# A convolution, a weighted sum over 49 neighbours and a whitening: weight loads on another queue, the sums of two images one gap later, and two softmaxes in another form

## The chip, the cores and the metric

The kernel runs on one core of a Trainium2 chip. It computes in float32. The metric is the device time of one execution in microseconds (us). Five engines work side by side, each on its own list of instructions in order: TensorE (PE: matmuls and transposes), VectorE (DVE), ScalarE (ACT), GpSimd (POOL) and SyncE (SP, which only issues DMAs). SP, ACT and POOL each can issue DMAs.

## The reference

Cut to what matters; x is (4, 256, 64, 64), so there are four images of 256 channels. They are counted 0 to 3 in this document, as the program does.

```python
# layer 0
k = conv(x, w1, padding=6, rhs_dilation=2) + b1         # 7x7, dilated by 2: 256 -> 128 channels
k = conv1x1(k, w2) + b2                                 # 128 -> 49
attn = softmax(k, axis=1)                               # 49 weights for each pixel
xp = pad(x, 6)
y[b,c,h,w] = sum over u,v in 0..6 of xp[b, c, h+2u, w+2v] * attn[b, 7u+v, h, w]
# layer 1: whitening of y, in 4 groups of 64 channels
Sigma = EPS*I + (yc @ yc.T) / m                         # yc: y less its mean over images and pixels
rTr = 1 / trace(Sigma);  P = I
for _ in range(5):
    P = 1.5*P - 0.5 * (P @ P @ P) @ (Sigma * rTr)
out = (P * sqrt(rTr)) @ yc * weight + bias
```

## The kernel before, in words

**Convolution.** The two convolutions of layer 0 have no function between them, so the kernel convolves with 49 outputs. It does so by evaluating input and weights at points and multiplying there, much as a Winograd algorithm does. The image is worked through in six row steps (`br` 0 to 5) with three banks each, by `conv_step`. A bank is one stretch of matmuls into PSUM (`conv_bank`, L599: 96, 80 and 32 matmuls in the three banks of a row), with operand `xh` (input values at the points) and weights `wr`. VectorE makes `rb`, `ct` and `xh` out of the image (L347, L350, L354, a few on ACT at L547), ACT copies the result out of PSUM into `pv` (L610, L615), and VectorE interpolates `pv` to `zz` and to the logits `lgx`. Weights at the points are made once and kept in DRAM (`gd`); every later image loads them back with `weights` (L419), 42 loads in all: 14 each of 588, 490 and 196 KB. Each of the three tags `wr0` to `wr2` has one buffer, so a load waits until the matmuls that used the last weights in it are done.

**Softmax.** `softmax(b, pc)` works on one image's pixels of one column parity `pc`. PE transposes the logits (L990), so that pixels lie on partitions; VectorE takes the maximum over 49 (L996) and turns its sign (L999). Then there are two forms. For images 0 to 2, ACT does 16 exps of 128x49 (L1016) with the maximum as bias and a sum as second output, which is an instruction of its own (ACTIVATION_READ_ACCUMULATOR). For image 3, VectorE adds the negated maximum (L1005, two instructions), ACT does two exps of 128x392 (L1012) and VectorE sums (L1013, two). In both, VectorE takes the reciprocal (L1020), masks it (L1022), multiplies (L1029) and shifts the terms between partitions with four shuffles (L1034).

**Weighted sums.** The sum over 49 neighbours is a matmul with a banded matrix for each of 16 pieces of work, n = 0 to 15, four for each image. `move_terms` copies the softmax terms into `zt` (on ACT, L1075, for images 0 to 2, and on VectorE, L1087, for image 3); POOL writes `zt` to DRAM (`sd`, L1092, eight DMAs); `load_band` reads it back on SP's queue as a band (L1127 `band`, L1138 `bandz`). `first_half(n)` and `second_half(n)` transpose blocks of the image (L1168), copy them out of PSUM (`xb` L1174, `xbz` L1182), multiply (`y`, L1210), store `y` (L1228 on VectorE, L1230 on ACT), turn it (L1241, copied by L1249 into `yt`), and add its moments for the whitening (`sig`, L1262). The copies of `xb` and half of the stores go to VectorE once the convolution of the last image is done (`tail`), and to ACT or by turns before.

**Order.** PE's order is that of the program. The convolution of image b + 1 has `NPC = 8` gaps, spread evenly by cost over its banks. `plan(b, j, f)` puts a piece of work into gap j of image b's convolution, and gaps past 7 run over into the next image or, behind the last, into the tail. Gaps 0 and 1 hold the two parts of the softmax of the image before. The eight halves of the sums of images 0 and 1 begin at gap 2 (past it for the following image), those of images 2 and 3 at gap 3. What is left at the end of the convolution of image 3 runs in the tail, in order. The other engines' lists are ordered by the scheduler of the framework, by its own estimates and by priorities. Layer 1's whitening and the output (`whiten`, L1594, L1610, L1561, L1563, L1598) follow the last sum.

The lines that set where things go:

```python
        if not first:
            nc.sync.dma_start(wt, gd[br][:, s0 : s0 + ns])          # weights(), L419
...
    for b in range(B):
        for j in range(2) if b else ():
            plan(b + 1, j, lambda b=b, j=j: soft(b, j))
```

Of the kernel before, what the change touches and what calls it, by code (L numbers as in the profile page):

```python
# [32 lines left out]
def kernel(  # L33
# [29 lines left out]
    nc = tc.nc  # L63
    B, C, H, W = x.shape
# [8 lines left out]
    NCH = SH // CR  # L73
# [21 lines left out]
    def taps(b):  # L95
        return (0,) if b == INF else (0, 1)
# [12 lines left out]
    def tp():  # L109
        return ps_tp.tile([P, 512], F32, tag="tp", name="tp")  # L110
# [72 lines left out]
    t = tp()  # L183
# [3 lines left out]
    t = tp()  # L187
# [4 lines left out]
    cv_buf = []  # L192
    for k in range(2):
        t = ps_cv.tile([P, 512], F32, name=f"cv{k}")
# [53 lines left out]
    for k, c0 in enumerate(range(0, P, CB)):  # L248
        n = min(CB, P - c0)
        t = cv_buf[k % 2]  # L250
# [15 lines left out]
    for k0 in range(0, KT, TB):  # L266
        n = min(TB, KT - k0)
        t = tp()
# [44 lines left out]
    for b in ORDER:  # L313
        slot_of[b] = nsl
        nsl += len(taps(b))
    gd = [
        dram.tile([P, nsl, NSK * len(taps(b)) // 2], F32, name=f"gd{b}") for b in range(NP)
    ]
# [27 lines left out]
    def add(o, a, b):  # L346
        return in_turn(TT(o, a, b, ALU.add))  # L347
# [57 lines left out]
    def weights(b, br, i, mid=None):  # L405

        first = (br, i) not in made
        made.add((br, i))
        s0 = slot_of[BANKS[i][0]]
        ns = sum(len(taps(bc)) for bc in BANKS[i])
        nk = NSK * len(taps(br)) // 2
        wt = apool.tile([P, ns, NSK], F32, tag=f"wr{i}", name=f"wr_{b}_{br}_{i}")[:, :, :nk]
        w = {bc: wt[:, slot_of[bc] - s0 : slot_of[bc] - s0 + len(taps(bc))] for bc in BANKS[i]}
        if not first:
            nc.sync.dma_start(wt, gd[br][:, s0 : s0 + ns])  # L419
            return w  # L420

        if br in kept:


            f = lgx if br == 4 else rb[0].rearrange("p q r c w -> p (q r c w)")
            f = f[:, : KS * nk]
            if i == 0:
                nc.sync.dma_start(f, kept[br])
            f = f.rearrange("p (v a r k) -> p v a r k", v=KS, a=NCC, k=KT)
            g = [f[:, v] for v in range(KS)]  # L430
        else:
            g = [gbr[:, v] for v in range(KS)]
        g = [t.rearrange("p a r k -> p (a r k)") for t in g]

        e = ct.rearrange("p a b -> p (a b)") if b else store[4].rearrange("p c r w -> p (c r w)")
        e, o, e1 = (e[:, k * nk : (k + 1) * nk] for k in range(3))
        g0 = [g[KS - 1 - a] for a in range(4)]
        g1 = [g[KS - 5 - a] for a in range(3)]
        o0 = {bc: w[bc][:, 0] for bc in w}
        o1 = {bc: w[bc][:, 1] for bc in w if bc != INF}  # L440

        def same(o, a):
            if br in kept:
                v = KS - 1 - a
                nc.sync.dma_start(o, kept[br][:, v * nk : (v + 1) * nk])
            else:
                nc.scalar.copy(o, g[KS - 1 - a])

        if i == 0:
            add(e, g0[0], g0[2])  # L450
            add(o, g0[1], g0[3])
            add(e1, g1[0], g1[2])
            add(o0[1], e, o)
            sub(o0[2], e, o)
            add(o1[1], e1, g1[1])
            sub(o1[2], e1, g1[1])
            same(o0[0], 0)
            same(o1[0], 4)
        elif i == 1:
            madd(e, g0[2], 4.0, g0[0])  # L460
            madd(o, g0[3], 4.0, g0[1])
            madd(e1, g1[2], 4.0, g1[0])
            madd(o0[3], o, 2.0, e)
            madd(o0[4], o, -2.0, e)
            madd(o1[3], g1[1], 2.0, e1)
            madd(o1[4], g1[1], -2.0, e1)
            same(o0[INF], 3)
        else:
            madd(o0[5], g0[0], 2.0, g0[1])
            madd(o1[5], g1[0], 4.0, g1[2])  # L470
            madd(o0[5], o0[5], 2.0, g0[2])
            if mid is not None:
                mid()
            madd(o1[5], g1[1], 2.0, o1[5])
            madd(o0[5], o0[5], 2.0, g0[3])
            add(o1[5], o1[5], o1[5])
        for bc in BANKS[i]:
            f = SCALE[bc] * (SCALE[br] if br not in kept else 1.0)
            if f != 1.0:
                nc.scalar.mul(w[bc], w[bc], f)  # L480
        nc.sync.dma_start(gd[br][:, s0 : s0 + ns], wt)
        return w
# [480 lines left out]
    NI = NCH // 2  # L963
# [16 lines left out]
    def softmax(b, pc):  # L980

        lv = logits[b].rearrange("p r w -> p (r w)")
        nm = f"{b}_{pc}"
        mx = work.tile([P, NCH, 2], F32, tag="mx", name=f"mx_{nm}")
        lt = []
        for hf in range(2):
            lt.append(tp().rearrange("p (i h k) -> p i h k", i=NI, h=2))
            for i in range(NI):
                pe(
                    nc.tensor.transpose(  # L990
                        lt[hf][:, i].rearrange("p h k -> p (h k)")[:, :K2],
                        lv[:K2, bass.ds(2 * (NI * hf + i) * P + pc, P, 2)],
                        ident[:K2, :K2],
                    )
                )
            nc.vector.tensor_reduce(  # L996
                mx[:, NI * hf : NI * (hf + 1)], lt[hf][:, :, :, :KT], AX.X, ALU.max
            )
        nc.vector.tensor_scalar(mx, mx, -1.0, None, ALU.mult)  # L999
        d = terms[b, pc] = bpool.tile([P, 2, NCH, KT], F32, tag="d", name=f"d_{nm}", bufs=2)  # L1000
        s = work.tile([P, 2, NCH], F32, tag="s", name=f"s_{nm}")
        if b == B - 1:
            for hf in range(2):
                half = slice(NI * hf, NI * (hf + 1))
                nc.vector.tensor_tensor(  # L1005
                    d.rearrange("p h i k -> p i h k")[:, half],
                    lt[hf][:, :, :, :KT],
                    mx[:, half].unsqueeze(3).to_broadcast([P, NI, 2, KT]),
                    ALU.add,
                )  # L1010
            for h in range(2):
                nc.scalar.activation(d[:, h], d[:, h], AF.Exp)  # L1012
                nc.vector.tensor_reduce(s[:, h], d[:, h], AX.X, ALU.add)  # L1013
        for h in range(2):
            for i in range(NCH) if b < B - 1 else ():
                nc.scalar.activation(  # L1016
                    d[:, h, i], lt[i // NI][:, i % NI, h, :KT], AF.Exp,
                    bias=mx[:, i, h : h + 1], accum_out=s[:, h, i : i + 1],
                )
            nc.vector.reciprocal(s[:, h], s[:, h])  # L1020
            rm = work.tile([P, NCH, KS], F32, tag="rm", name=f"rm_{nm}_{h}")
            nc.vector.tensor_tensor(  # L1022
                rm,
                s[:, h].unsqueeze(2).to_broadcast([P, NCH, KS]),
                cmask.unsqueeze(1).to_broadcast([P, NCH, KS]),
                ALU.mult,
            )
            dh = d[:, h].rearrange("p i (u v) -> p i u v", u=KS)
            nc.vector.tensor_tensor(  # L1029
                dh, dh, rm.unsqueeze(2).to_broadcast([P, NCH, KS, KS]), ALU.mult  # L1030
            )
        dv = d.rearrange("p h i (u v) -> p (h i u) v", u=KS)
        for step, vs in ((1, slice(4, 7, 2)), (2, slice(5, 7)), (-1, slice(0, 3, 2)), (-2, slice(0, 2))):
            last = nc.vector.stream_shuffle(  # L1034
                dv[:, :, vs], dv[:, :, vs], [(c - step) % SW for c in range(SW)]
            )

        return last
# [112 lines left out]
    tail = []  # L1151
# [177 lines left out]
    def bands(n, after=None):  # L1329

        move_terms(n, after)
        if n - 1 in half_done:
            load_band(n, 0)
        if n - 1 in done:
            load_band(n, 1)
            move_terms(n + 1, after)
# [26 lines left out]
    def plan(b, j, *what):  # L1363
        todo.setdefault((b + j // NPC, j % NPC), []).extend(what)

    def soft(b, pc):
        with tc.high_priority() if pc == 0 else nullcontext():
            last = softmax(b, pc)
        soft_done.add((b, pc))
        if pc == 0 and b == 0:  # L1370
            bands(0)

    for b in range(B):
        hs = [
            (lambda n=n, f=f: f(n))
            for n in range(4 * b, 4 * b + 4)
            for f in (first_half, second_half)
        ]
        if b + 2 < B:
            for j in range(8):  # L1380
                plan(b + 1, 2 + j, hs[j])
                if j == 3:

                    plan(b + 1, 2 + j, finish)
        else:
            for j in range(8):
                plan(b + 1, 3 + j, hs[j])
    for b in range(B):
        for j in range(2) if b else ():
            plan(b + 1, j, lambda b=b, j=j: soft(b, j))  # L1390
# [6 lines left out]
    for b in range(1, B):  # L1397
# [13 lines left out]
        j, at, whole = 0, 0, sum(c for c, _ in steps)  # L1411
# [242 lines left out]
```

## Time and profile before

| | |
|---|---|
| median of 3 runs (lowest, highest) | 739.77 us (734.72, 740.28) |
| the profiled execution: time, span | 736.93 us, 735.2 us |
| PE busy | 687.0 us, 93% of the span |
| VectorE busy | 594.5 us, 81% |
| ScalarE busy | 332.6 us, 45% |
| POOL busy | 133.2 us, 18% |
| convolution matmuls L599 | 234.1 us, 4160 of them |
| mean granted clock of PE | 0.974 |
| softmax of image 1 begins on PE | at 322.9 us of the span |
| softmax of image 2 begins on PE | at 469.0 us |
| convolution of image 3 ends on PE | at 562.0 us |

All stretches of time are in us from the start of the span. In a timeline row the first number is the start, the second the duration of the group; "x8" are eight instructions in it; what stands in square brackets is the engine's idle time before it and what it waited for. A row with "SPq" is SP's queue, where the duration includes the waits of the DMAs issued in that row. In a row of the costliest groups, "us, ns" are the sum and the mean of one.

### The profile page before, as it was taken

The numbers are of one execution on the slowest core, as the hardware profiler recorded it, in microseconds if no ns is written. First come the engines' busy times: TensorE is split into PE (matmuls) and PEld (weight loads), VectorE is DVE, ScalarE is ACT, GpSimd is POOL, SyncE is SP. The second block draws the span as 40 slices with busy tenths as digits, with TensorE's granted clock in tenths as the row PEclk, the third lists the DMA queues.
The fourth block names the chain that finished last, engine by engine and source line by source line (L and its number), as shares of the span: only waits on it lengthen the run. The fifth ranks groups of instructions, "written<-read, shape, count | busy, mean of one in ns | idle before, by whom it ended". The sixth has DMA issues, their size and how long they took to land.

```text
span 735.2 us, 19094 instructions
## 1 busy us (share of the span) xinstructions
PE 687.0 (93%) x7728; PEld 541.8 (74%) x7728; DVE 594.5 (81%) x1280; ACT 332.6 (45%) x930; POOL 133.2 (18%) x194
## 2 busy tenths in 40 slices
PE   6999999999898999988999999899999969997996
PEld 1449543478898988877999989898998858885231
DVE  3799998995796899989886899799959796435575
ACT  1424320133655654655555446727546422232564
POOL 0002526664031020020220200202202024200000
PEclk9999999999999999999999999999999978997899
DMA  8923999984665592147755820353623145463587
GB/s 321 260 91 105 238 364 234 224 184 91 174 170 146 209 292 68 62 131 252 214 128 187 279 69 11 98 163 76 182 83 79 45 89 130 107 249 140 235 362 319
DMA packets 78336, 126.09 MB, mean 172 GB/s; under 512 B 36471, under 2 KB 58664, under 8 KB 77096
## 3 DMA queue, kind: packets, MB, share of 16 engines
q1 hardware_dynamic: 65960, 82.79, 35.2%
q0 software_dynamic: 12288, 42.08, 22.1%
q8 instruction: 61, 1.00, 0.6%
q14 instruction: 27, 0.22, 0.1%
HBM read 78.78 MB, written 52.36 MB: 178 GB/s over the span
## 4 chain that ended last, share of the span: by engine, by line
PE 37%; DVE 26%; issue 9%; ACT 9%; POOL 4%; DMA 4%; SPq 0%; POOLq 0%; ACTq 0%; DVEq 0%
PE cv L599 16%; PE y L1210 6%; PE tp L1594 4%; DVE xh L354 3%; PE sig L1262 3%; DVE pv L354 3%; POOL ahead L147 3%; PE tp L1241 3%; DVE zz L354 2%; DMA band<-sd 2%; PE tp L1168 2%; DVE rb L347 2%; DVE rb L354 1%; ACT zt L1075 1%; POOL sd L1092 1%
## 5 line engine op out<-in xcount | busy, mean ns | idle before, releaser
L599 PE MATMUL cv<-xh,wr 128*49 128x128 f32 x4160 | 234.1, 275 | 0.0
L599 PEld LDWEIGHTS cv<-xh,wr 128*49 128x49 f32 x4160 | 229.1, 125 | 3.2 <-issue 1.3
L1092 POOL DMA_DIRECT2D sd<-zt x128 | 67.3, 533 | 310.5 <-ACT zt L1075 238.4
L1210 PE MATMUL y<-band,xb 128*128 128x209 f32 x512 | 113.0, 347 | 10.3 <-DMA band<-sd 10.1
L1210 PEld LDWEIGHTS y<-band,xb 128*128 128x128 f32 x512 | 87.5, 195 | 12.1 <-DMA band<-sd 9.1
L610 ACT COPY pv<-cv 113x486 f32<-113x486 f32 (+2 forms) x60 | 25.9, 432 | 98.4 <-PE cv L599 98.2
L1249 ACT COPY yt<-tp 128x256 f32<-128x256 f32 x128 | 45.5, 377 | 50.8 <-PE tp L1241 49.8
L1241 PE MATMUL tp<-ident,slot 128*128 128x128 f32 x256 | 52.4, 301 | 4.6 <-ACT yt L1249 3.0
L354 DVE SCALAR_TENSOR_TENSOR pv<-pv 113x162 f32<-113x162 f32 x176 | 52.9, 321 | 2.4 <-ACT pv L610 1.7
L1230 ACT ACTIVATE slot<-y,pivot 128x512 f32<-128x512 f32 x53 | 36.6, 739 | 35.6 <-PE y L1210 35.6
L1168 PE MATMUL tp<-ident,slot 128*128 128x128 f32 x256 | 50.2, 300 | 2.1 <-ACT xbz L1182 1.1
L1241 PEld LDWEIGHTS tp<-ident,slot 128*128 128x128 f32 x256 | 41.3, 205 | 12.5 <-ACT yt L1249 4.4
L1168 PEld LDWEIGHTS tp<-ident,slot 128*128 128x128 f32 x256 | 40.9, 204 | 5.9 <-ACT xbz L1182 1.4
L147 POOL DMA_DIRECT2D slot<-in_x_dram x20 | 33.9, 1695 | 51.4 <-issue 47.4
L1075 ACT COPY zt<-d 32x112 f32<-32x112 f32 (+2 forms) x132 | 38.2, 290 | 10.6 <-DVE d L1034 4.7
L354 DVE SCALAR_TENSOR_TENSOR xh<-ct 128x512 f32<-128x512 f32 x40 | 26.7, 689 | 18.5 <-PE cv L599 18.4
L1262 PE MATMUL sig<-yt 128*64 128x65 f32 x1024 | 37.5, 225 | 1.9 <-ACT yt L1249 1.9
L1262 PEld LDWEIGHTS sig<-yt 128*64 128x64 f32 x1024 | 32.8, 137 | 7.9 <-issue 4.1
L1016 ACT ACTIVATE d<-tp,mx 128x49 f32<-128x49 f32 x96 | 27.5, 332 | 19.2 <-DVE mx L999 19.2
L764 PE MATMUL acc<-slot,tap 128*49 128x256 f32 (+7 forms) x224 | 34.7, 468 | 0.0
L1174 ACT COPY xb<-tp 128x256 f32<-128x256 f32 x88 | 30.7, 377 | 8.1 <-PE tp L1168 7.8
L1228 DVE TENSOR_SCALAR slot<-y,pivot 128x512 f32<-128x512 f32 x11 | 8.3, 751 | 26.6 <-ACT slot L1230 26.6
(236 smaller groups left out, 1114.1 us busy)
## 6 DMA issues: line engine op xcount, KB each, us to landing
out_dram<-out SPq DMA_DIRECT2D x32, 512.0 KB, 3.6
band<-sd SPq DMA_DIRECT2D x64, 242.0 KB, 3.4
slot<-in_x_dram POOLq DMA_DIRECT2D x20, 512.0 KB, 7.3
sd<-zt POOLq DMA_DIRECT2D x128, 77.0 KB, 2.9
wr<-gd SPq DMA_DIRECT2D x14, 588.0 KB, 4.0
wr<-gd SPq DMA_DIRECT2D x14, 490.0 KB, 4.4
ahead<-in_x_dram POOLq DMA_DIRECT2D x12, 512.0 KB, 7.5
spill<-slot POOLq DMA_DIRECT2D x3, 2048.0 KB, 7.2
```

Source lines behind the costliest of these rows:

```text
L147: queue.dma_start(o[:, cc, h], src[:, :, pr, h * SW : (h + 1) * SW])
L354: return in_turn(STT(o, a, f, b, ALU.mult, ALU.add))
L599: nc.tensor.matmul(o, wv[:, sc, sr, cc], xv[bc][:, h * NCC + cc], start=(j == 0), stop=(j == len(terms) - 1), skip_group_check=True,)
L764: nc.tensor.matmul(ps[h * HB : h * HB + KT, :, o0:o1], w[v][:, cc], rhs, start=(j == 0 and k == 0), stop=(j == len(order) - 1), skip_group ...
L1075: ins = nc.scalar.copy(o, i)
L1092: nc.gpsimd.dma_start(bass.AP(tensor=D.tensor, offset=D.offset + h * HS + g * RS, ap=[[LS, TC], [CR * RS, NCH], [1, KS * WS]],), zt[p0 : p ...
L1168: nc.tensor.transpose(t[:, cc * P : (cc + 1) * P], tile_of(xt, cc, t8, h, pc), ident)
L1210: nc.tensor.matmul(ps[:, cc, q0 : q0 + nq, c0:c1], xb[:, cc * P : (cc + 1) * P], rhs, start=(k == 0), stop=(k == len(PIECES[half]) - 1), s ...
L1230: last = nc.scalar.activation(o, i, AF.Identity, bias=pivot[:, cc : cc + 1])
L1241: nc.tensor.transpose(t[:, cc * P : (cc + 1) * P], tile_of(yt, cc, i // 2, i % 2, pc), ident,)
L1249: return nc.scalar.copy(yb.rearrange("p a g c -> p (a g) c")[:, :, :GW], t[:, :C].rearrange("p (e c) -> p e c", c=GW),)
L1262: nc.tensor.matmul(sig[g * GW : (g + 1) * GW, cc], yb[:, cc, g, :GW], yb[:, cc, g], start=(count[0] == 0 and cc == 0), stop=(count[0] == 4 ...
```

## The change

There are five edits. Weights that are loaded back are issued on ScalarE's queue and no longer on SyncE's. The softmax of images 1 and 2 takes the form that image 3 has. The transposes of image 3's softmax go into the two PSUM buffers of the convolution (`cv_buf`), and not into those of `tp`. The sums of images 2 and 3 begin one gap later. And the first part of a softmax in the tail calls `bands` right away, so that the terms of n = 12 are moved at once.

```diff
@@ weights()
         if not first:
-            nc.sync.dma_start(wt, gd[br][:, s0 : s0 + ns])
+            nc.scalar.dma_start(wt, gd[br][:, s0 : s0 + ns])
             return w
@@ softmax(b, pc)
         for hf in range(2):
-            lt.append(tp().rearrange("p (i h k) -> p i h k", i=NI, h=2))
+            t = cv_buf[hf] if b == B - 1 else tp()
+            lt.append(t.rearrange("p (i h k) -> p i h k", i=NI, h=2))
             for i in range(NI):
...
-        if b == B - 1:
+        if b > 0:
             for hf in range(2):
...
         for h in range(2):
-            for i in range(NCH) if b < B - 1 else ():
+            for i in range(NCH) if b == 0 else ():
                 nc.scalar.activation(
@@ soft(b, pc)
         soft_done.add((b, pc))
-        if pc == 0 and b == 0:
-            bands(0)
+        if pc == 0 and (b == 0 or tail):
+            bands(4 * b)
@@ plan of the sums
         else:
             for j in range(8):
-                plan(b + 1, 3 + j, hs[j])
+                plan(b + 1, 4 + j, hs[j])
```

## The prediction

> **What bounds the kernel now.** I read the page first (engines, costliest groups), then the timelines of PE, SP and DVE around each softmax, and the windows of granted clock. All sums go against the profiled execution: span 735.2 us, whole run 736.93. The three runs have median 739.77; one per cent of that, 7.4 us, is about what a measurement here can tell from no change.
>
> ```profile
> PE 687.0 (93%) x7728; PEld 541.8 (74%) x7728; DVE 594.5 (81%) x1280; ACT 332.6 (45%) x930; POOL 133.2 (18%) x194
> ...
> L599 PE MATMUL cv<-xh,wr 128*49 128x128 f32 x4160 | 234.1, 275 | 0.0
> ...
> L1016 ACT ACTIVATE d<-tp,mx 128x49 f32<-128x49 f32 x96 | 27.5, 332 | 19.2 <-DVE mx L999 19.2
> ```
>
> TensorE (PE) sets the time, and its convolution (L599) never sat idle for an operand, a weight load included. So a gain can only come from PE's few holes. The softmax of image 1 shows the first kind:
>
> ```profile
> 321.91 0.45 PE L1262 MATMUL sig<-yt 128*64 128x65 f32 x8 [0.96 <-ACT yt L1249]
> ...
> 325.41 1.02 PE L990 MATMUL tp<-ident,lgx 113*128 113x113 f32 x4 [1.90 <-ACT xb L1174]
> 326.37 12.71 PE L599 MATMUL cv<-xh,wr 128*49 128x128 f32 x208
> ...
> 343.57 0.98 PE L1210 MATMUL y<-band,xb 128*128 128x209 f32 x4 [2.50 <-DMA band<-sd]
> ```
>
> Two waits for copies that stand on ACT between zt copies (L1075), and later one for a band. The band was late because SP serves one queue in order (first number start, second duration, x4 the four loads in it):
>
> ```profile
> 311.35 23.73 SPq L419 DMA_DIRECT2D wr<-gd  x4
> 335.24 0.81 SPq L1127 DMA_DIRECT2D band<-sd  x1
> ```
>
> Four weight loads hold SP for 23.73 us, each waiting for a PSUM bank's matmuls to be done with the old weights; the band stands behind, though its data had left POOL by 327.3. At image 2 the same (23.62 us from 457.44) costs nothing: its band is wanted later. The largest hole is in the tail, at sum n = 12:
>
> ```profile
> 593.80 1.15 PE L1262 MATMUL sig<-yt 128*64 128x65 f32 x32
> ...
> 602.93 1.76 PE L1210 MATMUL y<-band,xb 128*128 128x209 f32 x4 [5.15 <-DMA band<-sd]
> ...
> 613.46 1.15 PE L1262 MATMUL sig<-yt 128*64 128x65 f32 x32
> ...
> 627.63 1.15 PE L1262 MATMUL sig<-yt 128*64 128x65 f32 x32
> ```
>
> The sig moments (L1262) are my clock for the sums. From 613.46 to 627.63 is one n without a hole: 14.2 us, 7.9 for the first half and 6.3 for the second. From 593.80 to 613.46 is one first half that took 19.66: 11.8 lost, to a band that waits for the softmax of image 3 and to the half clock that followed (the columns are length, then busy us and count of PE, PEld, DVE, ACT and POOL, then the granted clock PEclk, the DMA share and GB/s):
>
> ```profile
> 585.00:598.42 13.42, 11.25 (x116) 9.58 (x116) 13.13 (x41) 4.68 (x10) 3.83 (x8) 1.00 0.17 28
> 598.42:612.07 13.65, 7.93 (x26) 6.66 (x27) 12.04 (x44) 0.74 (x2) 7.00 (x14) 0.50 0.71 155
> ```
>
> **The change part by part.**
>
> *Softmax of images 1 and 2.* Each of four calls loses 16 exps with 16 accumulator reads on ACT (pairs start about 0.28 us apart: 4.6 us) and gets two wide exps (0.53 each) there; VectorE gets two L1005 (0.52 apart) and two L1013 (0.55): 2.1 us, 8.4 in all. The zt copies no longer stand ahead of yt and xb in the changed order, so image 1's waits (0.96 + 1.90) go, and the half clock with them: 208 matmuls took 12.71 where 112 take 6.32 at full clock in the last stretch of the conv, so 208 would take 11.74; gain 1.0. VectorE's 2 x 2.1 per image lie in its lead: in the rows after this softmax its operand was ready 8.5 to 21.6 us before PE took it. If that lead were gone, the 4.2 would be on the path.
>
> *Weight loads on ACT.* 42 loads (14 each of 588, 490 and 196 KB) leave SP. Bands are then issued when their data is there: the wait of 2.50 goes. On ACT each load stands right behind the eviction of the bank that frees its buffer, so it seldom has to wait; some also wait on the completion of an earlier band (n = 0, 4, 8, 9), and evictions and the xb, xbz and yt copies are queued behind it, for which PE waits. Only n = 0's band is late enough, and PE waits for that band anyway; at most 3 us. The trace has no weight load issued on ACT. Bounds: 0 where ACT is idle (its share is 45%) to 0.53 (POOL's L1092 row, 533 ns). I take SP's own 0.33 (median of the L419 issues), as the queue kind is nearest: 42 x 0.33 = 13.9 us on ACT, of which I put 1.9 on the path before image 3, where first halves wait for ACT's xbz for 0.7 to 1.5 us now. So by the start of image 3's conv the shift is −(0.96 + 1.90 + 1.0 + 2.50) + 1.9 = −4.5 us; bounds −6.4 and about +1.
>
> The Trainium skill ("DMA: Bandwidth & Descriptors", "Issuing engines are not separate DMA queues") speaks against this part: moving issue to another engine only saves the sequencer's issue time. By that alone the move would be worth nothing to PE, and the shift −2.0; the 23.73 us above are a wait held in the queue, and not issue time, so I keep −4.5.
>
> *Sums of images 2 and 3 one gap later.* In image 3's conv, first half 8 moves behind the convolution of bank 0 of row (3,3), and second half 9 behind the conv's end. Image 2's softmax hole there holds 0.95 + 1.59 of waits plus 1.1 of half clock (416 matmuls in 24.58 us against 23.5): 3.6 us that go. But VectorE is barely ahead here: its operands were ready at 481.9, 488.5 and 500.0, PE took them at 486.6, 491.9 and 507.3. In the new order PE comes to the last one without first half 8 (9.1 us, 496.4 to 505.5): at 498.2 − 3.6 = 494.6. VectorE, with 4.2 more softmax of which its own idle here (2.58 us on 475.29) takes most, is ready at about 501.5 (bounds 500.0, nothing paid, and 504.2, all of it). PE stalls some 7 us, ends that bank (96 matmuls, 5.4) at 506.9, then does first half 8 (8.9 without its little wait): 515.8, where it stood at 512.7 before, so +3.1 in place of −3.6. With second half 9 (6.2) behind the end, the conv ends at 562.0 + 3.1 − 6.2 − 4.5 = 554.4.
>
> *The tail, counted from the conv's end.* Before: sig of first half 12 at +51.5 (613.46 − 561.96). After: second half 9 to +6.7; first half 10 with 1.2 of waiting for copies that now stand on VectorE behind the last logits (these were ready at +10.9) to +15.8; transposes of the first softmax part to +17.2 (into the conv's PSUM, which is free). Its chain on VectorE, from the rows at 578 to 595: maximum 1.1, negation 0.2, subtraction 1.0, wait for the exp 0.8, sums 1.1, reciprocal and mask 0.65, product 1.0, a store and two copies of the sums 1.5, shuffles 2.95, one maximum of the next part 0.5, zt 2.5: 13.4, done at +30.6. POOL's eight stores (4.3) and the band (about 3.4 from issue to landing) follow: the band of n = 12 is there by +40, before it is wanted; the old 5.15 us wait goes. But in the changed order the second part follows on VectorE at once, and the copy xb of n = 11's second block stands behind its products: 0.55 + 0.18 + 1.04 + 0.8 + 1.02 + 0.66 + 0.56 = 4.8, and 0.4 for the copy, +35.8. PE (second half 10 to +23.3, transposes, begin of first half 11) wants it at +27.4: a new wait of 8.4 us, followed by half clock as after 602.93. I put sig of first half 11 at +42.4 (without the wait some 32), second half 11 at +48.7, first half 12 at +56.6. That is 5.1 more than 51.5. Bounds: 46.2 if the copies slip past the softmax, 60 if the half clock lasts its full 13.65 us again.
>
> On the clock the Trainium skill ("TensorE: Matmul & The Clock Gate", Part 1) says that full speed returns after some 3.4 us of activity; the trace agrees for image 1 (3.41 us at 0.50) and not for n = 12 (13.65 us). By the rule the tail would come about 2 us earlier.
>
> **Sum:** −4.5 + 3.1 − 6.2 + 5.1 = −2.5. After n = 12 nothing changes (64.8 of the last 75 us are PE's). 736.93 − 2.5 = 734.4; the four executions shown average 737.9, 1.0 above the profiled one, so I predict 735.
>
> **Rivals.**
> A, *faster: no new wait in the tail.* If the xb copies of n = 11 run ahead of the second softmax part, sig of first half 12 comes at +46.2, and with ACT's issues hidden (−5.5): −5.5 + 3.1 − 6.2 − 5.3 = −14, so 723. For it: the old band wait has no other cause than order, and POOL and SP have time. Against: VectorE's queue runs in order, and the copy stands behind.
> B, *slower: ACT's queue pays for the loads.* Place: first halves between the conv's banks, where PE waits for ACT (xbz) already. Price: all 42 issues on the path at 0.33 = 13.9 instead of 1.9, so −2.5 + 12 = +9.5: 746. From 0.11 us of each on the path on (1.9 + 2.5 of 42), the change loses. Against: ACT's 45%, and 15 us of exps taken from it.
> C, *VectorE becomes the bound.* All of the 8.4 us are paid instead of the 1.5: −2.5 + 6.9 = +4.4: 741. Against: the lead of 8.5 us; for: the 3.4 to 4.8 at image 3.
> D, *the loads were hidden anyway:* PE never waits for weights, and the band's 2.50 us go to another wait: about 737.
>
> **How the numbers follow.** Forecast with D 0.47, A 0.21, B 0.20, C 0.12. The forecast's own range is 728 to 743. Faster by over 1% (below 732.4): A and the lower edge of the forecast, 0.26. Slower by over 1% (above 747.2): half of B and what several of the upper bounds together give, 0.20. Within: 0.54. The range reaches from A to a little above B: 722 to 748.
>
> **What would show it.** In the profile after: no L419 issue on SP beside the first ones; bands issued within 1 us of their data; no wait of PE for yt or xb above 0.5 us at image 1's softmax; PE stalled for VectorE's xh in row (3,3) of image 3, some 7 us; no band wait at n = 12; a wait for xb (L1174, VectorE) of some 8 us at n = 11 with half clock after it. The forecast is wrong if that last wait is missing (A), if PE's waits for ACT copies in first halves grow by over 5 us in total (B), or if L599 shows waits for xh in image 2's rows (C).

## The result, and the profile after

The change makes the kernel a little slower: 739.93 us against 737.52 (medians of 20 runs each), a ratio of 1.0032 with a 95% interval of 1.0016 to 1.0047. The forecast was 735, which came from a sum of 2.5 us less than the profiled execution of before; the time lies inside the range of 722 to 748 and inside "within 1%", but on the other side of no change. The profiled execution took 740.52 us (span 738.8), 3.6 more than that of before. Lines from 988 on have moved down by one in the changed kernel, so `y` is L1211, turning L1242, `sig` L1263, and so on. Ratios below are always to the kernel before, run beside on the same chip; 0.001 is 0.74 us.

The page after, engines and three groups:

```profile
PE 687.9 (93%) x7728; PEld 542.5 (73%) x7728; DVE 605.0 (82%) x1307; ACT 314.6 (43%) x799; POOL 133.2 (18%) x194
...
L599 PE MATMUL cv<-xh,wr 128*49 128x128 f32 x4160 | 233.1, 274 | 4.4 <-issue 4.4
...
L1211 PE MATMUL y<-band,xb 128*128 128x209 f32 x512 | 113.1, 348 | 8.1 <-DMA band<-sd 7.0
...
L1242 PE MATMUL tp<-ident,slot 128*128 128x128 f32 x256 | 51.6, 299 | 9.0 <-ACT yt L1250 6.7
```

VectorE gained 10.5 us of work (8.4 were counted for the softmax) and ScalarE lost 18.0. The convolution now has idle time ahead of its matmuls (4.4 us, 0.0 before), the bands cost 7.0 (10.1 before), and turning waits 6.7 for `yt` (3.0 before). So the waits have changed places more than they have grown or shrunk. PE's timeline around image 1's softmax shows where the forecast went wrong:

```profile
324.26 0.73 PE L991 MATMUL tp<-ident,lgx 113*128 113x113 f32 x4 [0.60 <-ACT xb L1175]
324.93 11.56 PE L599 MATMUL cv<-xh,wr 128*49 128x128 f32 x208
336.42 0.74 PE L1242 MATMUL tp<-ident,slot 128*128 128x128 f32 x4
338.49 0.98 PE L1211 MATMUL y<-band,xb 128*128 128x209 f32 x4 [1.32 <-DMA band<-sd]
...
342.75 1.31 PE L1211 MATMUL y<-band,xb 128*128 128x209 f32 x4 [2.82 <-DMA band<-sd]
```

The waits of 0.96 and 1.90 us for `yt` and `xb` have shrunk to 0.60, and the convolution stretch runs at full clock (11.56 us, 12.71 before). But the band waits have grown from 2.50 to 1.32 + 2.82, and half the clock follows for 3.41 us from 343.25. SP no longer holds the bands: it issues nothing between 303.5 and 335.7. POOL's timeline says what does; first before, then after:

```profile
323.08 4.21 POOL L1092 DMA_DIRECT2D sd<-zt  x8 [61.07 <-ACT zt L1075]
327.28 0.57 POOL L1280 DMA_DIRECT2D spill<-slot  x1
```

```profile
323.79 0.56 POOL L1281 DMA_DIRECT2D spill<-slot  x1 [60.22 <-ACT slot L1231]
326.01 3.72 POOL L1093 DMA_DIRECT2D sd<-zt  x7 [1.66 <-ACT zt L1076]
331.23 0.53 POOL L1093 DMA_DIRECT2D sd<-zt  x1 [1.50 <-DMA spill<-slot]
```

`spill` writes a finished 2 MB slot of `y` to DRAM (`move`). In the kernel before it stood behind the eight stores of the terms. Now it goes first, the terms are 2.9 us later, and the eighth store waits for the spill itself.

In the tail the place foretold has the wait foretold:

```profile
584.63 0.39 PE L1169 MATMUL tp<-ident,slot 128*128 128x128 f32 x2
590.92 0.70 PE L1242 MATMUL tp<-ident,slot 128*128 128x128 f32 x2 [5.91 <-ACT yt L1250]
593.05 0.70 PE L1169 MATMUL tp<-ident,slot 128*128 128x128 f32 x2 [1.42 <-DVE xbz L1183]
...
596.40 1.76 PE L1211 MATMUL y<-band,xb 128*128 128x209 f32 x4 [0.83 <-DVE xb L1175]
...
599.48 2.00 PE L1263 MATMUL sig<-yt 128*64 128x65 f32 x32
...
615.88 1.15 PE L1263 MATMUL sig<-yt 128*64 128x65 f32 x32
```

The three bracketed waits are 8.2 us in first half 11, with half clock from 589.01 to 602.66, and the last line is first half 12. The first of the waits passes through ScalarE, which the forecast had not named. Its timeline shows why: the exps of the second softmax part stand ahead of the `yt` copy and wait for VectorE's subtraction.

```profile
589.66 0.95 ACT L1013 ACTIVATE d<-d 128x392 f32<-128x392 f32 x2 [6.27 <-DVE d L1006]
590.52 0.35 ACT L1250 COPY yt<-tp 128x256 f32<-128x256 f32 x1
```

### The profile page after: what moved, and what is told of

Read it like the earlier page. It is cut to its first block, busy times and chain, and to the rows that moved or that the text cites. A ratio compares the mean times of both kernels' runs of the same rounds, so it can differ in the third digit from the quotient of the medians.

```text
span 738.8 us, 18995 instructions
## 1 busy us (share of the span) xinstructions
PE 687.9 (93%) x7728; PEld 542.5 (73%) x7728; DVE 605.0 (82%) x1307; ACT 314.6 (43%) x799; POOL 133.2 (18%) x194
## 4 chain that ended last, share of the span: by engine, by line
PE 38%; DVE 27%; issue 9%; ACT 5%; DMA 4%; POOL 4%; SPq 0%; ACTq 0%; POOLq 0%; DVEq 0%
PE cv L599 15%; PE y L1211 7%; PE tp L1595 4%; DVE xh L354 3%; PE tp L1242 3%; DMA band<-sd 3%; DVE pv L354 3%; PE sig L1263 3%; POOL ahead L147 2%; DVE zz L354 2%; PE tp L1169 2%; DVE rb L347 2%; DVE ct L354 1%; DVE rb L354 1%; DVE ct L347 1%
## 5 line engine op out<-in xcount | busy, mean ns | idle before, releaser
L1211 PE MATMUL y<-band,xb 128*128 128x209 f32 x512 | 113.1, 348 | 8.1 <-DMA band<-sd 7.0
L1211 PEld LDWEIGHTS y<-band,xb 128*128 128x128 f32 x512 | 87.4, 194 | 10.0 <-DMA band<-sd 5.6
L1242 PE MATMUL tp<-ident,slot 128*128 128x128 f32 x256 | 51.6, 299 | 9.0 <-ACT yt L1250 6.7
L1242 PEld LDWEIGHTS tp<-ident,slot 128*128 128x128 f32 x256 | 41.2, 205 | 15.9 <-ACT yt L1250 7.8
L1263 PE MATMUL sig<-yt 128*64 128x65 f32 x1024 | 38.6, 231 | 0.0
L1263 PEld LDWEIGHTS sig<-yt 128*64 128x64 f32 x1024 | 34.0, 143 | 5.8 <-issue 4.4
L354 DVE SCALAR_TENSOR_TENSOR xh<-ct 128x512 f32<-128x512 f32 x40 | 26.4, 688 | 13.7 <-PE cv L599 13.7
L1175 ACT COPY xb<-tp 128x256 f32<-128x256 f32 x82 | 28.6, 375 | 13.9 <-PE tp L1169 13.2
L764 PEld LDWEIGHTS acc<-slot,tap 128*49 128x49 f32 x224 | 16.1, 123 | 17.9 <-issue 14.9
```

Of the source, the lines that this page charges most:

```text
L354: return in_turn(STT(o, a, f, b, ALU.mult, ALU.add))
L764: nc.tensor.matmul(ps[h * HB : h * HB + KT, :, o0:o1], w[v][:, cc], rhs, start=(j == 0 and k == 0), stop=(j == len(order) - 1), skip_group ...
L1211: nc.tensor.matmul(ps[:, cc, q0 : q0 + nq, c0:c1], xb[:, cc * P : (cc + 1) * P], rhs, start=(k == 0), stop=(k == len(PIECES[half]) - 1), s ...
L1242: nc.tensor.transpose(t[:, cc * P : (cc + 1) * P], tile_of(yt, cc, i // 2, i % 2, pc), ident,)
L1263: nc.tensor.matmul(sig[g * GW : (g + 1) * GW, cc], yb[:, cc, g, :GW], yb[:, cc, g], start=(count[0] == 0 and cc == 0), stop=(count[0] == 4 ...
```

## The experiments

Theory 1 held that the change traded one wait for another at two places: the band of n = 4 (behind the weight loads on SP before, behind the spill on POOL after), and the tail's first half 11 (behind the softmax). Theory 2, its rival, was that 42 loads on ScalarE and VectorE's longer softmax cost time everywhere. Line numbers of these kernels differ by a few from those above. Rows without "before +" also hold the change's two other edits (image 3's transposes in the convolution's PSUM, the terms of n = 12 moved at once); no run tries these two by themselves.

| kernel | weights on | softmax 1, 2 | sums from gap | also | ratio (95% interval) |
|---|---|---|---|---|---|
| changed | ACT | new | 4 | | 1.0032 (1.0016 to 1.0047) |
| e13 | ACT | old | 3 | before + this alone | 0.9993 (0.9972 to 1.0015) |
| e14 | SP | new | 3 | before + this alone | 0.9927 (0.9900 to 0.9953) |
| e4 | SP | new | 4 | | 0.9993 (0.9975 to 1.0011) |
| e5 | ACT | new | 3 | | 0.9980 (0.9957 to 1.0004) |
| e6 | ACT | old | 4 | | 1.0011 (0.9990 to 1.0033) |
| e1 | ACT | new | 4 | spill on SP | 1.0025 (1.0008 to 1.0043) |
| e10 | ACT | new | 4 | spill held back | 0.9956 (0.9934 to 0.9978) |
| e11 | SP | old | 3 | before + spill held back | 0.9989 (0.9963 to 1.0015) |
| e18 | ACT | new | 3 | spill held back | 0.9929 (0.9907 to 0.9950) |
| e19 | SP | new | 3 | before + form + spill held back | 0.9924 (0.9899 to 0.9948) |
| e2 | ACT | new | 4 | softmax part 2 later | 1.0001 (0.9980 to 1.0023) |
| e15 | ACT | new | 4 | e2 + tail copies on ACT | 0.9913 (0.9882 to 0.9945) |
| e16 | ACT | new | 4 | e15 + spill held back | 0.9866 (0.9831 to 0.9901) |
| e17 | ACT | new | 3 | e16, sums early | 0.9837 (0.9799 to 0.9875) |

### The spill on another queue (e1)

```diff
-            nc.gpsimd.dma_start(spill[k], slots[k]...)
+            nc.sync.dma_start(spill[k], slots[k]...)
```

> The changed kernel, with the three stores of finished image slots (spill, 2 MB each) issued on SP's queue instead of POOL's; SP is free since the weight loads left it. Theory 1 (a wait replaced a wait): in the changed kernel the bands of n = 4 came late (waits of 1.32 and 2.82 us, and 3.4 us of half clock behind them) because POOL issued the spill ahead of the softmax terms, and the last of the eight term stores waited for the spill to land. Then both waits go, the half clock too, and the time falls by 4 to 6 us against the changed kernel, to about 735. Theory 2 (ScalarE's weight issues and VectorE's longer softmax cost time everywhere, and the band is incidental): the time stays within 1 us of the changed kernel, 739 to 741.

Measured: 740.54 us, no gain; theory 1 in this form failed. The eighth store no longer waits, the terms leave POOL in one run from 324.47 to 328.68, and the bands are late all the same: PE waits 1.08 and 2.76 us. The DMA issues from 318 to 345 us (last number: median us from issue to landing) say that it is not the queue. Before, changed, e1:

```profile
sd<-zt POOLq DMA_DIRECT2D x8, 77.0 KB, 2.6
```

```profile
sd<-zt POOLq DMA_DIRECT2D x8, 77.0 KB, 6.9
```

```profile
sd<-zt POOLq DMA_DIRECT2D x8, 77.0 KB, 6.5
```

The same eight stores take 2.6 us to land with the spill behind them and 6.5 to 6.9 with it ahead. Theory 3 followed: what is late is bytes, whatever queue issues them.

### The spill held back (e10, e11)

The one spill of image 1 is put behind the term stores of n = 5 on POOL, by an order within that queue:

```diff
+                sd_last[n] = nc.gpsimd.dma_start(            # the term stores
...
+            dma = nc.gpsimd.dma_start(spill[k], slots[k]...)
+            if k == 1:
+                tc.add_manual_dep(dma.ins, sd_last[5].ins.name, ...)
```

> The changed kernel, with the one spill store that runs at image 1's softmax (2 MB, slot 1) held back on POOL's queue until the terms of n = 5 are written, some 30 us later. Moving it to SP's queue (the run before) had left the band waits of n = 4 at 1.08 and 2.76 us. Theory 3 (the band waits for bytes, not for a queue): the 16 DMA engines are 0.8 to 0.98 busy from 324 to 336 us with spill, weights and terms, so terms and bands land late whatever queue issues them; with the spill held back both waits and the half clock behind them go, 4 to 5.5 us, to about 735. Rival: the weight loads alone keep the engines full or the bands come late for another reason: within 1.5 us of 739.9.

Measured: 0.9956, so 0.0076 less than the changed kernel, 5.6 us (some 2 either way). In the two profiled executions PE goes from the `sig` ahead of image 1's softmax to that of first half 4 in 22.97 us, where the changed kernel took 27.06: 4.1 us are seen at this place. PE's timeline of e10:

```profile
334.88 0.74 PE L1243 MATMUL tp<-ident,slot 128*128 128x128 f32 x4
336.92 0.98 PE L1212 MATMUL y<-band,xb 128*128 128x209 f32 x4 [1.30 <-DMA band<-sd]
...
338.57 0.98 PE L1212 MATMUL y<-band,xb 128*128 128x209 f32 x4 [0.20 <-DMA band<-sd]
```

Of 4.14 us of waiting, 1.50 are left, and no half clock follows (none before 492.85). The DMA engines' share in this stretch (second number from the end; GB/s last) falls, first the changed kernel, then e10:

```profile
324.00:328.00 4.00, 3.74 (x60) 3.63 (x62) 4.00 (x7) 2.56 (x9) 2.33 (x5) 1.00 0.81 344
328.00:332.00 4.00, 4.00 (x78) 4.00 (x76) 4.00 (x14) 0.95 (x2) 2.26 (x5) 1.00 0.98 289
```

```profile
324.00:328.00 4.00, 4.00 (x78) 4.00 (x74) 4.00 (x8) 1.08 (x4) 3.83 (x8) 1.00 0.58 119
328.00:332.00 4.00, 4.00 (x78) 4.00 (x76) 4.00 (x14) 2.09 (x4) 0.37 (x1) 1.00 0.57 107
```

The spill is not all that delays the terms: without it the eight stores take 4.8 us to land here, with the weight loads on ScalarE, and 2.7 in e11, with the loads on SP. What makes up the rest was not tested.

The same in the kernel before:

> The kernel before, with the same spill store held back until the terms of n = 5 are written; weights stay on SP's queue. Theory 3: the wait of 2.50 us for the band of n = 4 shrinks to 0.5 us or less although the bands still stand behind four weight loads on SP: 735, 2 to 2.5 us faster. The step of the prediction (SP's queue makes the band late): the wait stays at 2 us or more, and the time at 737.6.

Measured: 0.9989, and the wait stays:

```profile
341.63 0.98 PE L1211 MATMUL y<-band,xb 128*128 128x209 f32 x4 [2.66 <-DMA band<-sd]
```

SP's timeline has the cause, a fifth weight load between the two halves of the band, and the four ahead as before:

```profile
309.37 23.73 SPq L419 DMA_DIRECT2D wr<-gd  x4
333.27 0.37 SPq L1128 DMA_DIRECT2D band<-sd  x1
...
337.15 0.33 SPq L419 DMA_DIRECT2D wr<-gd  x1
337.66 0.56 SPq L1128 DMA_DIRECT2D band<-sd  x1
```

So theory 3 was half right, and so was the prediction. There are two limits on this band, SP's queue and the spill's bytes. With the weights on SP, holding the spill back brings nothing (e11); with the spill ahead, moving the weights brings nothing (e13, below); with both gone, the changed kernel gains 5.6 us.

### The weight loads (e4, e13, e18, e19)

> The changed kernel, with the weight loads back on SP's queue; softmax form, later sums and transposes into the conv's PSUM stay. Theory 1: the bands of n = 4 are late either way (behind the weights on SP here, behind the spill on POOL there), and 42 issues of 0.33 us on ScalarE cost PE little: 738 to 741, no difference. Theory 2 (ScalarE's queue pays): 3 us or more faster than the changed kernel, 737 or less.

Measured: 0.9993, some 2.9 us faster than the changed kernel; between the two expectations, nearer to the second. In this kernel POOL again writes the terms first (322.29) and the spill behind them (326.49). That is so in the three kernels with weights on SP and no hold on the spill (before, e4, e14); in the six with weights on ScalarE and the spill free on POOL (changed, e2, e5, e6, e13, e15) the spill is first. What goes with it is ScalarE's order: in the changed kernel `yt` and `xb` copies stand ahead of zt copies, and the terms begin to leave POOL 4.6 us after the last `sig` ahead of the softmax (e13 4.8), where it was 3.1 before (2.0 in e4).

> The kernel before, with only the weight loads moved to ScalarE's queue. From the run with the weights back on SP (2.2 us faster than the changed kernel) the move alone costs about 2 us: 739 to 740.5. By the prediction's sum (bands earlier by 2.50, 1.9 us of issues on the path) it gains: 735 to 737.

Measured: 0.9993, no difference. The trace has both sides of the trade, with the old softmax form: the waits at the softmax are down to 0.73 us for `xb`, and those for the band up to 1.21 + 3.14.

> The changed kernel with its sums back at gap 3 and the spill store held back behind the terms of n = 5: so weights on ScalarE, the new softmax form, and no spill in front. If the spill is all that the weight loads cost, it is as fast as the softmax form alone or faster by the freed band wait: 0.987 to 0.993 of the kernel before. If the issues on ScalarE cost too: 0.995 or more (0.998 was measured with the spill ahead).

Measured: 0.9929, the same as the new softmax form alone (e14, 0.9927), though e18 has the freed band as well. So it lies in the range of the first expectation, but does not show that the issues on ScalarE are free.

> The kernel before with the new softmax form alone and the spill store held back; weights on SP. Theory 3 with two limits (SP's queue and the spill's bytes): the band of n = 4 still waits behind the weight loads, 2 to 3 us, and the time is that of the softmax form alone within 0.3%: 0.990 to 0.996. If only the bytes counted: 0.985 to 0.988.

Measured: 0.9924; PE waits 0.40 + 1.79 us for the band. Both as expected from two limits.

The two limits can be read from all 16 profiled executions, in us on PE:

| stretch | loads on SP | loads on ScalarE, spill not held | loads on ScalarE, spill held |
|---|---|---|---|
| `sig` ahead of image 1's softmax to that of first half 4 | 27.8 to 28.7 (before, e4, e11, e14, e19) | 26.4 to 28.2 (changed, e1, e2, e5, e6, e13, e15) | 22.3 to 23.0 (e10, e16, e17, e18) |
| from there to the `sig` ahead of image 2's softmax | 118.3 | 119.0 to 119.3 | 119.0 |

The first row is the band: only where both limits are gone is the stretch shorter. The second row is a price of the loads on ScalarE, 0.7 us, so this half of theory 2 is small but not nothing. And the freed band is not yet a faster run than one with the loads on SP: e18 is 5.8 us ahead of e19 at image 2's softmax (461.03 and 466.84), but its run is not shorter (0.9929 and 0.9924). In the two profiles 0.9 us go in image 3's convolution and 3.4 behind it, where e18 has half clock for 17.07 + 17.07 us and e19 for 6.83 + 13.65. How much of that belongs to the loads was not tested.

### The softmax form (e6, e14)

> The changed kernel, with the softmax of images 1 and 2 in its old form (16 exps and 16 accumulator reads on ScalarE for each part). By the prediction the new form is worth 3.9 us at image 1 and up to 3.6 at image 2, less what VectorE is late there: 742 to 744 without it. If the waits that left were a matter of the order on ScalarE alone, or if VectorE's 8.4 us cost as much as they bring: 739 to 741.

Measured: 1.0011, not slower than the changed kernel at all: the credit of 3.9 + 3.6 us could not be found there.

> The kernel before, with only the softmax form of images 1 and 2 changed (VectorE adds and sums, two wide exps on ScalarE). The prediction credits this part with PE's waits for yt and xb and the half clock behind them, 3.9 us at image 1 and 3.6 at image 2: 0.99 to 0.993 of the kernel before. Rival: those waits are set by where the zt copies stand on ScalarE, which came with the weight loads (the run with the weights moved alone had already lost them), and the exps of 4.6 us are hidden: 0.997 to 1.003, with the waits of 0.96 and 1.90 us still there.

Measured: 0.9927, 5.4 us faster, near what the prediction allowed, but not by the waits that it named. With the new form and the loads on SP most of the `xb` wait of 1.90 at image 1 stays (e14, first row; e4 and e19 have 1.59 and 1.58), and what falls is that for `yt`, from 0.96 to 0.26. With the loads moved and the old form the `xb` wait falls to 0.73 (e13, second row; e6 has 0.70) and that for `yt` goes:

```profile
323.75 0.73 PE L990 MATMUL tp<-ident,lgx 113*128 113x113 f32 x4 [1.60 <-ACT xb L1174]
```

```profile
324.63 0.73 PE L990 MATMUL tp<-ident,lgx 113*128 113x113 f32 x4 [0.73 <-ACT xb L1174]
```

What e14's trace shows of the gain lies later: from the `sig` ahead of image 2's softmax to the end of image 3's convolution PE takes 93.2 us, where it took 95.9 before. With the sums at gap 4 and the loads on ScalarE the form brings nothing there (91.2 in the changed kernel, 91.1 in e6): PE comes earlier and waits longer for `xh` (4.11 us, 3.73 in e6), until 500.3 in both. That is why e6 finds no credit. The other half of e14's 5.4 us is not located: its profiled execution took 736.92 us, the upper end of its 12 runs (730.78 to 736.92).

### The later sums, and the tail (e5, e2, e15, e16, e17)

> The changed kernel, with the sums of images 2 and 3 back at gap 3. Theory 1: PE's stall of 4.1 us for xh in image 3's convolution goes, second half 9 is back inside the convolution, and the tail has one half less to cover the softmax with, so the band wait at n = 12 or a block at n = 11 is longer by about that half: 738 to 740. Theory 2 (the later sums are what costs): 736 or less, as the stall of 4.1 us is gone without a return.

Measured: 0.9980, 3.8 us less than the changed kernel; between the two again. The long stall for `xh` is gone and the band wait at n = 12 is back (5.91 us).

> The changed kernel, with the second part of image 3's softmax planned one gap later, behind first half 11 instead of ahead of it. Theory 1: PE's block at n = 11 in the tail (waits of 5.91, 1.42 and 0.83 us, then half clock for 13.65 us) comes from copies of xb on VectorE and of yt on ScalarE that stand behind the second softmax part; with that part later, at most 3 us of it are left (the copies then stand behind the zt copies of the first part), and the time falls by 5 to 8 us, to about 733. Theory 2: the block only takes the place of the band wait at n = 12 and something else takes its place again (the band of n = 13, which becomes ready later): within 1.5 us of 740.

```diff
-            plan(b + 1, j, lambda b=b, j=j: soft(b, j))
+            plan(b + 1, j + (b == B - 1) * j, lambda b=b, j=j: soft(b, j))
```

Measured: 1.0001, 2.3 us less than the changed kernel, where 5 to 8 were expected. The wait at n = 11 fell to 3.78 us, behind the zt copies; 3.9 us of new waits for `xb` and `xbz` appeared at n = 12 and 1.18 for the band at n = 13. VectorE's queue was still the limit, so the next run takes the copies out of it:

```diff
+        on_v = tail and n >= 13
-            (nc.vector.tensor_copy if tail else nc.scalar.copy)(xb, t[:, :C])
+            (nc.vector.tensor_copy if on_v else nc.scalar.copy)(xb, t[:, :C])
```

> The changed kernel, with the second part of image 3's softmax behind first half 11 (as in the run before with that alone, which left waits of 3.78 us behind the zt copies and of 1.63, 1.18 and 1.04 us at n = 12), and the copies xb and xbz of n = 10 to 12 on ScalarE, not VectorE, in the tail. Theory 1 (the tail's block is VectorE's queue): first half 12's sig comes 47 to 50 us after the convolution's end instead of 57.2, and the time is 7 to 10 us below the changed kernel: 0.990 to 0.994 of the kernel before. Rival: terms or bands of n = 12 and 13 become the wait: 0.998 or more.

Measured: 0.9913, 8.8 us less than the changed kernel. First half 12's `sig` comes at 607.48, 48.0 us after the end of the convolution (57.2 in the changed kernel); the waits that remain are for bands:

```profile
584.07 0.98 PE L1212 MATMUL y<-band,xb 128*128 128x209 f32 x4 [0.76 <-DMA band<-sd]
587.08 1.76 PE L1212 MATMUL y<-band,xb 128*128 128x209 f32 x4 [1.56 <-DMA band<-sd]
...
592.75 1.15 PE L1264 MATMUL sig<-yt 128*64 128x65 f32 x32
...
607.48 1.15 PE L1264 MATMUL sig<-yt 128*64 128x65 f32 x32
```

> As e15, and the spill store at image 1's softmax held back behind the terms of n = 5. If the two places are independent, the gains add: 5.6 of the spill and 7 to 10 of the tail, 0.982 to 0.987 of the kernel before. If a later wait absorbs one of them: 0.99 or more.

Measured: 0.9866, 3.5 us below e15, where the spill alone gave 5.6 on the changed kernel (each some 2 to 3 us either way): the two places add, nearly or fully.

> As e16, with the sums of images 2 and 3 back at gap 3 as in the kernel before. If moving the sums later costs more in image 3's convolution (PE stalls 4.1 us for xh, half clock behind it) than it gives in the tail: 2 to 4 us faster than e16. If the half that lies in the tail is needed to cover the softmax of image 3: 1 to 5 us slower than e16, with a band wait at n = 12.

Measured: 726.59 us, 0.9837, 2.1 us below e16 (both intervals overlap). This is the fastest version tried: weights on ScalarE, the new softmax form, the spill held back, the tail's copies on ScalarE, and the sums where they were before. A wait of 5.15 us for the band of n = 12 is left in it.

## Why the prediction was wrong

Its sum can be laid beside the two profiled executions, term by term, in shifts of PE's time in us (after less before):

| step of the prediction | forecast | measured |
|---|---|---|
| up to image 1's softmax | (in the 1.9 below) | +1.3 (320.03 to 321.37) |
| waits and half clock at image 1's softmax | −3.9 | −3.9 (convolution stretch ends at 336.49, was 339.08) |
| the band of n = 4 | −2.5 | +3.2 (`sig` at 348.43, was 347.82) |
| from there to image 2's softmax, ScalarE's issues | +1.9 | +0.7 (467.44, was 466.12) |
| image 3's convolution, to the end of first half 8 | +3.1 | +1.5 (515.53, was 512.74) |
| second half 9 behind the convolution | −6.2 | −6.1 (it ends at 558.68, was 562.00) |
| tail to first half 12 | +5.1 | +5.7 (57.2 against 51.5) |
| sum at first half 12 | −2.5 | +2.4 |
| whitening (half clock for 17.07 us, was 13.65) | 0 | +1.2 |

**The step that failed** is the one on the weight loads: "Bands are then issued when their data is there: the wait of 2.50 goes." It was 5.7 us off in the profile, more than the whole difference of 4.9. SP's queue did hold the band (e11 shows it), but it was not the only thing that did: in the changed order a spill of 2 MB goes first, and the terms and the band move beside it (share of the DMA engines 0.81 and 0.98, without the spill 0.58 and 0.57). e10 holds it back and gains 5.6 us; at image 2's softmax PE is then at 461.83, 4.3 us ahead of before, where the prediction had said 4.5. That these two agree is in part luck: the band gives 0.9 there and not 2.5, and the issues cost 0.7 and not 1.9. The prediction had read POOL's row to see when the terms left it, and had not looked at what stood in POOL's list behind them, or asked whether it would still stand there. It also took the four loads of 23.73 us for what held the band. The band load that PE waited for stood behind a fifth weight load, which came only when the convolution's stretch ended at 339.1:

```profile
339.12 0.33 SPq L419 DMA_DIRECT2D wr<-gd  x1
339.63 0.66 SPq L1127 DMA_DIRECT2D band<-sd  x1
```

The prediction did name the outcome, in rival D ("the band's 2.50 us go to another wait"), but with no place and as part of its forecast.

**ScalarE's issues** were priced at 1.9 us, and at 13.9 in rival B. The traces show 0.7 up to image 2's softmax (119.0 against 118.3); for the later stretch the price is open, and no run comes near rival B. The +1.3 ahead of the softmax is no cost of theirs: it is half clock at 230.61, behind two waits that the kernel before has too (below), and e10 and e18, with the same issues, don't have it. (In rival A the prediction writes −5.5 for the shift with the issues hidden; its own terms add to −6.4. Nothing else rests on it.)

**The softmax form** was given about the right size at image 1 and, in the main, the wrong owner. The sum of 3.9 us came out, but 0.60 us of the `xb` wait is left, and most of what went left with the loads: e13 and e6 lose it with the old form, and e4, e14 and e19 keep 1.58 to 1.60 with the new one. Alone the form gives 5.4 us, of which the trace shows 2.7, and these at image 2 and 3.

**Image 3's convolution and the tail** were read rightly, with one size off: the convolution cost 1.5 and not 3.1. It stalled (4.11 + 0.30 us, where 7 were forecast) at the row named; PE came at 496.2 and not 494.6, and went on at 500.3, not 501.5. The profile names no releaser for this wait; VectorE finished an `xh` 0.1 us before its end (L347, 0.68 us from 499.50).

```profile
482.87 13.31 PE L599 MATMUL cv<-xh,wr 128*49 128x128 f32 x240 [0.30 <-issue]
500.29 2.13 PE L599 MATMUL cv<-xh,wr 128*49 128x128 f32 x17 [4.11 <-issue]
```

(The second row is cut off at 502 us, where the view ends.)

The old band wait at n = 12 fell from 5.15 to 0.93 us, and the new block at n = 11 came with 8.2 us where 8.4 were forecast, with half clock for 13.65 us. Its cause is confirmed by e15, which takes the copies out of VectorE's queue, orders the softmax later and gains 8.8. That the block reached PE first through `yt` on ScalarE was missed. e2, which only delayed the softmax part, gave less than expected because the copies still stood on VectorE behind the zt copies (3.78 us).

The half-clock rows also bear on the rule that the prediction weighed: in the tail full speed took 13.65 us to return, as before, and 3.41 in e15, where PE's waits were short. So these traces show no one fixed time.

The last row of the table, in which nothing should have changed, and the first are half clock that other kernels here have or lack whatever their edits (17.07 us in the whitening in seven of the 16 profiles, 13.65 in nine). Together they are 2.5 of the 3.6 us between the two profiles. The medians of 20 runs differ by 2.4 (1.2 to 3.5); the terms that belong to the change account for 1.1 of it in this pair, and where the rest lies is not shown.

What stays open is why moving the loads changes ScalarE's order so that the terms come later than the spill. It is seen in all six kernels with the loads on ScalarE and the spill free on POOL, but the scheduler's reasons weren't tested.

## What to carry to other kernels

When a transfer is late, list everything that it needs in order, each queue that it passes and the bytes that go beside it, and price the removal of one limit by the next one, not by the wait that is seen. Look at what stands around the late transfer's own producers in the changed order, on every queue, and not only on the queue from which something was taken. And try each part of a change alone: here one part alone was worth 5.4 us, and the kernel with all five edits was 2.4 us slower than the one with none.

## What was not expected of the hardware

Half clock begins on a fixed grid in the changed kernel's trace: at 230.61, 343.25, 500.26 and 589.01 us, which lie 33, 46 and 26 times 3.413 us apart. The same waits can fall on either side of it. Between 227.6 and 230.7 PE waits 1.09 and 0.78 us for `xbz`, in every kernel here at about that place; in the profiled execution of the changed one the grid cut off a stretch in which PE was busy 1.63 of 3.42 us, and the next ran at half speed:

```profile
227.19:230.61 3.42, 1.63 (x9) 0.98 (x7) 3.39 (x5) 3.07 (x9) 0.00 (x0) 1.00 0.16 54
230.61:234.02 3.41, 3.33 (x38) 3.03 (x39) 1.60 (x5) 1.35 (x3) 0.00 (x0) 0.50 0.81 259
```

In that of before the waits are the same to 0.01 us and no half clock follows. So one profiled execution carries shifts of 1 to 2 us at a place that are no part of the change, and a single pair of traces can't settle a term of that size; that the spread of one kernel's runs (734.61 to 741.45 for the kernel before) comes from this is likely, but was not shown.
